# A graph network layer in f32: aggregated rows through DRAM at register-held addresses, and 16 gathers from x in the head

## The chip, the cores and the metric

The kernel runs on one core of a Trainium2 chip. The metric is device time in microseconds of one execution, the median of several. A core has five engines that work from queues of their own: PE (matrix multiplication, PEld being its weight loads), DVE (vector), ACT (activation functions), POOL (GpSimd, which here issues the gathers) and SP (which here only issues DMA transfers and, after the change, loads registers). The engines run in order, each for itself, and wait for one another by semaphores.

## The reference

A message-passing layer over a graph of 6250 nodes with 256 features and 206250 edges. The edges come sorted by their target `dst`. Everything is f32.

```
h   = relu(layernorm(x))                                    # per node
e   = relu(raw @ W_e1.T + b_e1) @ W_e2.T + b_e2             # raw: 64 features per edge
emb = (e * (clip(pol, 0, 1) + 0.01)) @ W_le.T + b_le
msg = relu(h[src] + emb)                                    # a gathered row of h per edge
agg = segment_sum(msg, dst, 6250)
g   = (h + agg) @ W_g1.T + b_g1
out = x + relu(layernorm(g) * ln_g + ln_b) @ W_g2.T + b_g2
```

The edges per node average 33; the sums per node are what the change touches.

## The kernel before

**Edges.** 128 edges are a tile, 4 tiles (512 edges) a *block*, 403 blocks in all; half a block, 256 edges, is a *unit*, 806 in all. Six blocks are a *group* `g` of 3072 edges, 68 groups in all. A group is cut into four *strips* of 768 consecutive edges, and tile `j` of each block belongs to strip `j`. A strip's edges have targets within `W` = 32 consecutive nodes, beginning at the strip's first target, `base_b[:, g, j]`. A test on the chip checks this; where it fails, a general loop (`any_order`, L845) does the layer again at the end.

**Per unit.** `first_layer` (L239, matmul L250, ReLU on ACT L259 and DVE L256) makes the hidden layer of two blocks, `edge_part` (L266, matmul L274) multiplies by the product of the second and third weights, DVE moves the result out of PSUM (`msg`, L279). POOL gathers two tiles of 128 rows of `hb_d` (the normalized nodes with a bias added, in DRAM) into `hg` by indirect DMAs (`gather`, L566). `whole(u)` (L607) then makes the message: DVE multiplies `msg` by the polarity and adds `hg` (L615), ACT takes the ReLU (L620). `add_up` (L622, matmul L632) sums messages into 4 x 32 rows of PSUM per group with a 0/1 matrix; `keep` (L639) copies a finished group's rows to `ms[g]` (L644).

**Per node window.** 128 nodes are a *window* `w`, 49 in all. A window can get rows from two or three groups (`groups_of`, L71). `node_work` (L680) loads x transposed (L691) and its statistics (L693), makes h from them (L707, four DVE instructions), builds one 128 x 128 selection matrix per group (L698), and sums the groups' rows into the window's nodes on PE (L732: two halves of the features, a matmul per group and half), adds them (L734), and goes through `first` (matmul L170, L176), `second` (transposes L186) and `third` (matmul L196, result L198). A matmul in f32 is recorded as two.

**The order** is written out by hand (`manual_schedule`). A loop over the units (L785) places each unit's steps on all engines: `at(u, fn)` puts a step of the node work at a later unit, `steps` and `rest` are small pieces for DVE, taken one per unit by `piece` (L600). PE runs ahead of the gathers: the first `LEAD` = 22 units go through PE while the head still computes `hb_d`, and `whole` follows a lag behind (L793), which starts at `LEAD - RAW` = 18 units and falls by one every `SHRINK` = 44 units. For eight units in a row the sums and first layers are done together (`turn_of`, L291).

**The gathers.** A gather is placed behind a matmul (`in_step`, L578): while the gathers so far times `STEP` = 1.288 are less than the estimated PE time `spent` plus `AFLOAT`. `spent` adds up given costs per step (`EDGE`, `LAYER`, `SUMS`, `NODES`; the last for every step that `due` takes). `whole` places the ones it still lacks with no such wait (L796). There are `HG` = 20 buffers of one unit, and L582 lets no gather go beyond 20 units past those already summed.

**The head** (L355 to 475). Until `hb_d` is written no gather can read it, so the first `RAW` = 4 units gather rows of x itself (8 gathers, L347) and normalize them after gathering (L464, L472, L611 in `whole`). x comes in 13 chunks through 11 buffers (`p1x`), 10 of them asked for at once (`AHEAD`); per chunk DVE takes the statistics (L141, L142), ACT applies them (L388), POOL adds the bias (L392) and SP writes `hb_d` (L394).

Of the kernel before, what the change touches and what calls it, by code (L numbers as in the profile page):

```python
# [17 lines left out]
P = 128  # L18
# [16 lines left out]
NT = NB * S  # L35
NG = NF + 1
NP = -(-NB // 2)
MARGIN = 768
DEG = E // N
LEAD = 22  # L40
# [1 line left out]
EDGE, LAYER, SUMS, NODES = 1.754, 0.9, 0.46, 0.65  # L42
STEP = 1.288
AFLOAT = 6.0
SHRINK = 44
RAW = 4
HG = 16 + RAW
FEW = 6
QUIET = (0, 1)
TURN = 1  # L50
CH = 4
AHEAD = 10
assert DEG * N == E and NF * GE + S * P >= E


# [42 lines left out]
def gnn_kernel(ctx: ExitStack, tc: tile.TileContext, x, src_c, dst_c, dst_r, pol_c, raw_t, w_e1t, w_e2,  # L98
# [50 lines left out]
    def finish_nodes(nd, ps, w, n):  # L149

        r = w * P

        def turn(a):
            pt = ps()
            for c in range(2):
                nc.tensor.transpose(pt[:, 0, c * P:c * P + n], a[:n, c * P:(c + 1) * P], ident[:n, :n])
            aT = nd.tile([P, 2, P], F32, name="aT")
            if n == P:
                nc.scalar.activation(aT, pt[:, 0, :].rearrange("p (c n) -> p c n", c=2), AF.Copy)
            else:  # L160
                for c in range(2):
                    nc.scalar.activation(aT[:, c, :n], pt[:, 0, c * P:c * P + n], AF.Copy)
            return aT

        def first(aT, bias_by_pe=False):
            ph = ps()
            if bias_by_pe:
                nc.tensor.matmul(ph[:n, 0, :], ones[0:1, :n], bg1_b[0:1], start=True, stop=False)
            for c in range(2):
                nc.tensor.matmul(ph[:n, 0, :], aT[:, c, :n], wg1_s[:, c, :], start=c == 0 and not bias_by_pe, stop=c == 1)  # L170
            hs = nd.tile([P, D], F32, name="hs")
            if bias_by_pe:
                hb = ph[:, 0, :]
            else:
                hb = hs
                nc.vector.tensor_add(hs[:n], ph[:n, 0, :], bg1_b[:n])  # L176
            mv = row_stats(nd, n, 1, lambda i: hb[:n])
            rs = nd.tile([P, 1], F32, name="rs1")
            one_over_std(rs[:n], mv, n)
            nc.vector.tensor_scalar(hs[:n], hb[:n], mv[:n, 0, 0:1], rs[:n], op0=ALU.subtract, op1=ALU.mult)  # L180
            return hs

        def second(hs):
            pt = ps()
            for c in range(2):
                nc.tensor.transpose(pt[:, 0, c * P:c * P + n], hs[:n, c * P:(c + 1) * P], ident[:n, :n])  # L186
            nT = nd.tile([P, 2, P], F32, name="nT")
            for c in range(2):
                nc.scalar.activation(nT[:, c, :n], pt[:, 0, c * P:c * P + n], AF.Relu, bias=lnb_s[:, c:c + 1],  # L189
                                     scale=lng_s[:, c:c + 1])  # L190
            return nT

        def third(nT, xt):
            po = ps()
            for c in range(2):
                nc.tensor.matmul(po[:n, 0, :], nT[:, c, :n], wg2_s[:, c, :], start=c == 0, stop=c == 1)  # L196
            ot = nd.tile([P, D], F32, name="ot")
            nc.vector.tensor_add(ot[:n], po[:n, 0, :], xt[:n])  # L198
            for i, (a, b) in enumerate(spread_out(n)):
                eng = nc.scalar if i else nc.sync  # L200
                eng.dma_start(out=out[bass.ds(r + a, b - a), :], in_=ot[a:b])

        def load_x():
            xt = nd.tile([P, D], F32, name="xt3")
            for a, b in spread_out(n):
                nc.sync.dma_start(out=xt[a:b], in_=x[bass.ds(r + a, b - a), :])
# [11 lines left out]
    with fast:  # L218
# [297 lines left out]
        ends = w0.tile([P, 3], F32, name="ends")  # L516
        bad = w0.tile([P, 3], F32, name="bad")
        bad3 = w0.tile([3, 1], F32, name="bad3")

        def by_group(i, op):  # L520
            def step():
# [17 lines left out]

        def count():  # L540
            pq = ps()
            nc.tensor.matmul(pq[:3, 0, 0:1], bad, ones[:, 0:1], start=True, stop=True)
            nc.vector.tensor_copy(bad3, pq[:3, 0, 0:1])

        def total():
            pq = ps()
            nc.tensor.matmul(pq[:1, 0, 0:1], bad3, ones[0:3, 0:1], start=True, stop=True)
            nc.vector.tensor_copy(bad_i, pq[:1, 0, 0:1])


        with tc.tile_pool(name="hg", bufs=HG - RAW) as hg_p, tc.tile_pool(name="ms", bufs=5) as ms_p, \
                tc.tile_pool(name="sel2", bufs=9) as sel2_p, tc.tile_pool(name="nd", bufs=3) as nd:
            got = 2 * RAW
            acc = {}
            made = 0
# [83 lines left out]
            def keep(g):  # L639

                if g is not None:
                    ms[g] = ms_p.tile([P, D], F32, name="ms")
                    if g != NG - 2:
                        nc.scalar.activation(ms[g], acc.pop(g), AF.Copy)  # L644
# [29 lines left out]
            rest = deque()  # L674
            ending = {-2: [], -1: []}

            def at(u, fn):
                todo.setdefault(max(u, now), deque()).append(fn)

            def node_work(w, spread_now=False):  # L680
# [6 lines left out]

                def spread():
                    box["xt"] = load_x()
                    box["hT"] = nd.tile([P, 2, P], F32, name="hT")  # L690
                    nc.sync.dma_start(out=box["hT"][:, :, :n], in_=x_t[:, :, w * P:w * P + n])  # L691
                    st = nd.tile([P, 2, P], F32, name="stb")
# [88 lines left out]
            for i, fn in enumerate((by_group(0, ALU.max), by_group(1, ALU.min), by_row(0, ALU.max), by_row(1, ALU.min),  # L781
                                    verdict, count, total)):
                at(LEAD + 22 + 5 * i, fn)
            flag = None
            for u in range(LEAD, NU):  # L785
# [9 lines left out]
                while made < ready_for:  # L795
                    gathers(made + 1)  # L796
                    whole(made)
                    made += 1
                due()
                if len(rest) > 6:  # L800
                    piece()
                if u == NU - 24:
# [1 line left out]
                        if groups_of(w)[-1] == NG - 1:  # L804
                            late[w] = node_work(w, True)
                if u == LEAD + 60:
                    flag = nc.values_load(bad_i[0:1, 0:1], min_val=0, max_val=3 * P)
            while todo:
                now = min(todo)
                for fn in todo.pop(now):  # L810
                    fn()
            while steps:
                steps.popleft()[1]()
            before, last = ending[-2], ending[-1]
# [192 lines left out]
```

## Time and profile before

| | us |
|---|---|
| median of 3 runs | 2162.19 (2161.35 to 2164.05) |
| the profiled execution, its own time | 2161.02 |
| its span, first to last instruction | 2159.3 |
| busy in the span: PE | 2144.8 |
| busy: DVE, POOL, ACT | 1665.9, 1621.5, 980.5 |
| gathers from `hb_d` (POOL, L566) | 1604, mean 983 ns |
| L732, matmuls that sum groups' rows into windows | 548 records, 69.3 busy |

The profile lists for each group of instructions its line, engine, operation and tiles, the count behind an x, then busy time, mean duration of one in ns, and behind the second bar the engine's idle time just before them with what ended most of it. In a timeline the columns are start and duration in us; in square brackets stands the idle time before and its releaser. Busy time of PE is modelled, and issuing a DMA or loading a register is not counted as busy.

### The profile page before, as it was taken

Reading aid. Unit: us, or ns where it says so; the run is one execution under the profiler, and the core shown is the slowest. Engines: PE = TensorE matmul, PEld = TensorE weight load, DVE = VectorE, ACT = ScalarE, POOL = GpSimd, SP = SyncE. Lnnn points to the kernel's source line nnn. Section 1 sums busy time; section 2 is a strip of 40 time slices with the busy share of each in tenths; the row PEclk is TensorE's granted clock in tenths of the full one; section 3 lists DMA queues with packets and bytes.
Section 4 is the critical chain, followed back from the end, with each engine's and each line's share of the span. In section 5 each row is a group of like instructions: output and inputs, shape, how many; then the busy total and the mean of one; then the engine's idle time right before and its main releaser. Section 6 shows DMA issues by size and latency. Waiting matters only on the chain.

```text
span 2159.3 us, 35666 instructions
## 1 busy us (share of the span) xinstructions
PE 2144.8 (99%) x12382; PEld 1613.3 (75%) x12382; DVE 1665.9 (77%) x3975; ACT 980.5 (45%) x1710; POOL 1621.5 (75%) x1675
## 2 busy tenths in 40 slices
PE   9999999999999999999999999999999999999998
PEld 6677777777777777777777777777777777777776
DVE  7898777877777777777777777778777778777786
ACT  7544444444444444444444444444444444444443
POOL 6777777777777777777777777777777777777773
PEclk9999999999999999999999999999999999999999
DMA  9544454544445454545454445444544554454442
GB/s 312 175 134 127 141 157 135 150 137 131 140 131 148 144 149 125 152 131 149 124 151 142 133 130 153 143 133 141 147 138 125 150 151 140 128 152 131 140 138 73
DMA packets 156227, 309.23 MB, mean 143 GB/s; under 512 B 33328, under 2 KB 78089, under 8 KB 156041
## 3 DMA queue, kind: packets, MB, share of 16 engines
q0 software_dynamic: 77376, 211.39, 34.6%
q1 hardware_dynamic: 77364, 92.23, 13.6%
q10 hardware_dynamic: 1300, 3.28, 0.5%
q8 instruction: 98, 1.61, 0.3%
q14 instruction: 89, 0.72, 0.1%
HBM read 293.92 MB, written 12.85 MB: 142 GB/s over the span
## 4 chain that ended last, share of the span: by engine, by line
PE 96%; DVE 2%; DMA 1%; ACT 0%; issue 0%; SPq 0%; DVEq 0%; ACTq 0%
PE pz L274 64%; PE pz L250 17%; PE pd L632 9%; PE pz L732 3%; PE pz L170 2%; PE pz L196 2%; DMA raw<-in_raw_t_dram 1%; PE pz L186 1%; DVE hg L615 0%; DVE msg L279 0%; DVE st L141 0%; DMA xt<-in_x_dram 0%; DVE sel L595 0%; DVE mvx L142 0%; DVE msg L613 0%
## 5 line engine op out<-in xcount | busy, mean ns | idle before, releaser
L566 POOL DMA_INDIRECT hg<-hb_d,src_s x1604 | 1576.6, 983 | 493.9 <-issue 319.8
L274 PE MATMUL pz<-wc_s,e 128*128 128x256 f32 x6448 | 1452.6, 381 | 0.0
L274 PEld LDWEIGHTS pz<-wc_s,e 128*128 128x128 f32 x6448 | 1209.5, 190 | 235.2 <-ACT e L259 71.3
L620 ACT ACTIVATE hg<-hg 128x512 f32<-128x512 f32 x805 | 507.6, 631 | 862.7 <-DVE hg L615 860.9
L615 DVE SCALAR_TENSOR_TENSOR hg<-msg,pol_s,hg 128x256 f32<-128x256 f32 x1612 | 696.8, 477 | 15.6 <-DMA hg<-hb_d,src_s 14.9
L279 DVE TENSOR_TENSOR msg<-pz,bc_s 128x512 f32<-128x512 f32 x799 | 545.5, 683 | 74.0 <-PE pz L274 73.7
L256 DVE TENSOR_SCALAR e<-pz,vecs 128x512 f32<-128x512 f32 x201 | 150.8, 750 | 361.1 <-PE pz L250 361.0
L259 ACT ACTIVATE e<-pz,vecs 128x512 f32<-128x512 f32 x605 | 361.1, 691 | 148.4 <-PE pz L250 148.3
L250 PE MATMUL pz<-raw,we_s 64*128 64x512 f32 x1612 | 379.3, 604 | 3.7 <-DVE msg L279 2.0
L250 PEld LDWEIGHTS pz<-raw,we_s 64*128 64x128 f32 x1612 | 148.5, 187 | 188.2 <-issue 155.4
L632 PE MATMUL pd<-hg,sel 128*32 128x256 f32 x3216 | 194.9, 382 | 0.6 <-ACT hg L620 0.6
L632 PEld LDWEIGHTS pd<-hg,sel 128*32 128x32 f32 x3216 | 94.4, 109 | 87.8 <-issue 34.9
L595 DVE SCALAR_TENSOR_TENSOR sel<-iota_w,zero_c,rel 128x128 f32<-128x128 f32 x403 | 137.3, 341 | 0.0
L644 ACT ACTIVATE ms<-pd 128x256 f32<-128x256 f32 x66 | 25.2, 382 | 127.2 <-PE pd L632 127.1
L732 PEld LDWEIGHTS pz<-s,ms 128*128 128x128 f32 x548 | 68.7, 192 | 3.1 <-PE pd L632 0.4
L732 PE MATMUL pz<-s,ms 128*128 128x128 f32 x548 | 69.3, 275 | 0.1
L707 DVE SCALAR_TENSOR_TENSOR hT<-hT,zero_c,stb 128x128 f32<-128x128 f32 (+1 forms) x196 | 66.7, 341 | 3.0 <-DMA stb<-st_d 3.0
L196 PE MATMUL pz<-wg_s,nT 128*128 128x256 f32 (+1 forms) x196 | 50.6, 380 | 0.6 <-ACT nT L189 0.6
L170 PE MATMUL pz<-wg_s,hT 128*128 128x256 f32 (+1 forms) x196 | 50.5, 380 | 0.0
L392 POOL TENSOR_TENSOR hb<-xt,rows_b 128x256 f32<-128x256 f32 (+1 forms) x49 | 34.1, 728 | 10.5 <-ACT xt L388 3.0
L196 PEld LDWEIGHTS pz<-wg_s,nT 128*128 128x128 f32 (+1 forms) x196 | 37.0, 190 | 6.2 <-ACT nT L189 0.8
L170 PEld LDWEIGHTS pz<-wg_s,hT 128*128 128x128 f32 (+1 forms) x196 | 37.0, 190 | 5.7 <-issue 0.3
(98 smaller groups left out, 412.8 us busy)
## 6 DMA issues: line engine op xcount, KB each, us to landing
raw<-in_raw_t_dram SPq DMA_DIRECT2D x202, 256.0 KB
hg<-hb_d,src_s POOLq DMA_INDIRECT x1604
stb<-st_d SPq DMA_DIRECT2D x49, 128.0 KB
hb_d<-hb SPq DMA_DIRECT2D x12, 512.0 KB
xt<-in_x_dram SPq DMA_DIRECT2D x48, 128.0 KB
hT<-in_x_t_dram SPq DMA_DIRECT2D x48, 128.0 KB
out_dram<-ot SPq DMA_DIRECT2D x48, 128.0 KB
xt<-in_x_dram SPq DMA_DIRECT2D x11, 512.0 KB
```

The costliest lines, as they stand in the source:

```text
L196: nc.tensor.matmul(po[:n, 0, :], nT[:, c, :n], wg2_s[:, c, :], start=c == 0, stop=c == 1)
L250: z = nc.tensor.matmul(pe[s, c], we1_s[s * F:(s + 1) * F, c * P:(c + 1) * P], raw[q][s * F:(s + 1) * F, :], start=True, stop=True)
L256: nc.vector.tensor_scalar(e1[b][:, c, :], pe[s, c], be1_s[:, c:c + 1], 0.0, op0=ALU.add, op1=ALU.max)
L259: nc.scalar.activation(e1[b][:, c, :], pe[s, c], AF.Relu, bias=be1_s[:, c:c + 1])
L274: last_z = nc.tensor.matmul(pz[:, i, :], e1[b][:, c, k:k + P], wc_s[:, c, :], start=c == 0, stop=c == 1)
L279: nc.vector.tensor_add(msg[u], pz, bc_s)
L566: g = nc.gpsimd.indirect_dma_start(out=hg[u][:, i, :], out_offset=None, in_=hb_d, in_offset=bass.IndirectOffsetOnAxis(ap=src_s[:, 2 * u + ...
L595: nc.vector.scalar_tensor_tensor(sel[g][:, k * S:(k + 1) * S, :], iota_w.rearrange("p (o w) -> p o w", o=1).to_broadcast([P, S, W]), zero_ ...
L615: nc.vector.scalar_tensor_tensor(hg[u][:, i, :], m[:, i, :], pol_s[:, 2 * u + i:2 * u + i + 1], hg[u][:, i, :], op0=ALU.mult, op1=ALU.add)
L620: nc.scalar.activation(hg[u], hg[u], AF.Relu)
L632: z = nc.tensor.matmul(acc[g][j * W:(j + 1) * W, :], sel[g][:, k * S + j, :], m[:, j % 2, :], start=k == 0, stop=b == blocks_of(g)[-1])
L732: nc.tensor.matmul(pa[:, c, :n], ms[g][:, c * P:(c + 1) * P], box["sel2"][i][:, :n], start=i == 0, stop=i == len(gs) - 1)
```

## The change

For the windows whose last group is below `FAR` = 66 (47 of 49) the sums take another way.

- **Rows to DRAM** (`rows_out`). When a group below 66 is finished, SP loads the first rows of its four strips into registers and writes each strip's 32 rows of `ms[g]` to DRAM at that row: strips 0 and 2 to `sum_d[0]`, 1 and 3 to `sum_d[1]`, so that neighbours, which can share nodes, never write the same array. Both arrays are cleared window by window some groups ahead (`clear`, from a tile of zeros). A new term of the test (`strips_apart`) checks that strips two apart begin at least 32 rows apart.
- **Rows back** (`far_work`, instead of `node_work`). Per window: x is loaded one unit after the window's last group, h is made from it on ACT four units after, and the window's 128 rows of both arrays are read; six units after, DVE adds both to h; nine units after, PE transposes the result (two transposes, `turn`, L153) and ACT copies it; then `first`, `second` and `third` as before. Gone for these windows are the selection matrices, L691, L693, L707, L732 and L734.
- **The head.** `RAW` is 8: 16 gathers of x instead of 8, their statistics and normalization with them, and eight gathers from `hb_d` fewer. `HG` stays 20. x goes through 9 buffers instead of 11, 8 asked for at once. The lag starts at 22 - 8 = 14 units and falls by one every 57 units.
- Buffers: `ms` 4 instead of 5, `sel2` 6 instead of 9, new pools for the rest.

```diff
-SHRINK = 44
-RAW = 4
-HG = 16 + RAW
+SHRINK = 57
+RAW = 8
+HG = 20
-AHEAD = 10
+AHEAD = 8
+CLEAR = 4
+FAR = NG - 2
...
+    sum_d = [dram.tile([N + W, D], F32, name=f"sum_d{i}") for i in range(2)]
...
-        def turn(a):
+        def turn(a, pool=nd, name="aT"):
...
-        with tc.tile_pool(name="p1", bufs=4) as p1, tc.tile_pool(name="p1x", bufs=11) as p1x:
+        with tc.tile_pool(name="p1", bufs=4) as p1, tc.tile_pool(name="p1x", bufs=9) as p1x:
...
+            nc.vector.tensor_copy(base_i, base_b[0:1].rearrange("p g j -> p (g j)"))
+            nc.vector.memset(zrow, 0.0)
...
+        def strips_apart():
+            flat = base_b.rearrange("p g j -> p (g j)")
+            n = FAR * S - 2
+            nc.vector.tensor_tensor(apart[:, :n], flat[:, 2:n + 2], flat[:, :n], ALU.subtract)
+            nc.vector.tensor_reduce(ends[:, 3:4], apart[:, :n], axis=AX.X, op=ALU.min)
...
+            nc.vector.tensor_scalar(bad[:, 3:4], ends[:, 3:4], float(W), None, op0=ALU.is_lt)
...
-                if steps and steps[0][0] <= now:
-                    steps.popleft()[1]()
+                due_now = [s for s in steps if s[0] <= now][:1]
+                if due_now:
+                    steps.remove(due_now[0])
+                    due_now[0][1]()
...
+                    if g < FAR:
+                        soon(1, lambda: rows_out(g, 0))
+                        soon(2, lambda: rows_out(g, 1))
                     for w in range(NW):
-                        if groups_of(w)[-1] == g:
+                        if groups_of(w)[0] == g + CLEAR:
+                            soon(6, lambda w=w: clear(w))
+                        if groups_of(w)[-1] == g < FAR:
+                            far_work(w)
+                        elif groups_of(w)[-1] == g:
                             late.pop(w)()
-                        elif groups_of(w)[-1] == g + 1 < NG - 1:
+                        elif groups_of(w)[-1] == g + 1 == FAR:
                             late[w] = node_work(w)
...
+            def soon(n, fn):
+                moves.setdefault(now + n, []).append(fn)
+
+            def clear(w):
+                if groups_of(w)[-1] < FAR:
+                    for i in range(2):
+                        nc.sync.dma_start(out=sum_d[i][w * P:(w + 1) * P, :], in_=zrow)
+
+            def rows_out(g, k):
+                if k == 0:
+                    _, firsts[g] = nc.values_load_multi_w_load_instructions(
+                        base_i[0:1, g * S:(g + 1) * S], engines=[mybir.EngineType.SP], min_val=0, max_val=N)
+                for i in range(2):
+                    j = 2 * k + i
+                    nc.sync.dma_start(out=sum_d[i][bass.ds(firsts[g][j], W), :], in_=ms[g][j * W:(j + 1) * W, :])
+
+            def far_work(w):
+                box = {}
+                turn, first, second, third, load_x, offset = finish_nodes(nd, ps, w, P)
+
+                def h_of_x():
+                    box["xt"] = load_x()
+                    box["h"] = nh.tile([P, 2, P], F32, name="stb").rearrange("p a b -> p (a b)")
+
+                def load():
+                    nc.scalar.activation(box["h"], box["xt"], AF.Relu, bias=nm_s[:, w:w + 1], scale=rs_s[:, w:w + 1])
+                    box["ab"] = ab_p.tile([P, 2, D], F32, name="ab")
+                    for i in range(2):
+                        nc.sync.dma_start(out=box["ab"][:, i, :], in_=sum_d[i][w * P:(w + 1) * P, :])
+
+                def add(i):
+                    nc.vector.tensor_add(box["h"], box["h"], box["ab"][:, i, :])
+
+                def turned():
+                    box["hT"] = turn(box["h"], nh, "hT")
+                    at(now + 2, one)
...
+                soon(1, h_of_x)
+                soon(4, load)
+                steps.extend((now + 6, lambda i=i: add(i)) for i in range(2))
+                steps.extend((now + 7, lambda c=c: offset(box["xt"], c)) for c in range(2))
+                at(now + 9, turned)
...
+            now = LEAD
+            for w in range(NW):
+                if groups_of(w)[0] < CLEAR:
+                    soon(8, lambda w=w: clear(w))
...
                 due()
+                for fn in moves.pop(now, []):
+                    fn()
```

More of the change, by code (lines that the diff above doesn't have):

```diff
@@ L156, in turn @@
                 nc.tensor.transpose(pt[:, 0, c * P:c * P + n], a[:n, c * P:(c + 1) * P], ident[:n, :n])
-            aT = nd.tile([P, 2, P], F32, name="aT")
+            aT = pool.tile([P, 2, P], F32, name=name)
             if n == P:
@@ L512, in row_numbers @@
                 nc.vector.tensor_scalar(rowid[q], base_b[q, :, j], p32[q], None, op0=ALU.add)
+            nc.vector.tensor_copy(base_i, base_b[0:1].rearrange("p g j -> p (g j)"))
+            nc.vector.memset(zrow, 0.0)
         far = w0.tile([P, 2, NG], F32, name="far")
-        ends = w0.tile([P, 3], F32, name="ends")
-        bad = w0.tile([P, 3], F32, name="bad")
-        bad3 = w0.tile([3, 1], F32, name="bad3")
+        ends = w0.tile([P, 4], F32, name="ends")
+        bad = w0.tile([P, 4], F32, name="bad")
+        bad4 = w0.tile([4, 1], F32, name="bad4")
+        apart = w0.tile([P, FAR * S], F32, name="apart")
         def by_group(i, op):
@@ L538, in verdict @@
             nc.vector.tensor_scalar(bad[:, 2:3], ends[:, 2:3], float(GE // 2 + MARGIN), None, op0=ALU.is_gt)
+            nc.vector.tensor_scalar(bad[:, 3:4], ends[:, 3:4], float(W), None, op0=ALU.is_lt)
         def count():
             pq = ps()
-            nc.tensor.matmul(pq[:3, 0, 0:1], bad, ones[:, 0:1], start=True, stop=True)
-            nc.vector.tensor_copy(bad3, pq[:3, 0, 0:1])
+            nc.tensor.matmul(pq[:4, 0, 0:1], bad, ones[:, 0:1], start=True, stop=True)
+            nc.vector.tensor_copy(bad4, pq[:4, 0, 0:1])
         def total():
             pq = ps()
-            nc.tensor.matmul(pq[:1, 0, 0:1], bad3, ones[0:3, 0:1], start=True, stop=True)
+            nc.tensor.matmul(pq[:1, 0, 0:1], bad4, ones[0:4, 0:1], start=True, stop=True)
             nc.vector.tensor_copy(bad_i, pq[:1, 0, 0:1])
-        with tc.tile_pool(name="hg", bufs=HG - RAW) as hg_p, tc.tile_pool(name="ms", bufs=5) as ms_p, \
-                tc.tile_pool(name="sel2", bufs=9) as sel2_p, tc.tile_pool(name="nd", bufs=3) as nd:
+        with tc.tile_pool(name="hg", bufs=HG - RAW) as hg_p, tc.tile_pool(name="ms", bufs=4) as ms_p, \
+                tc.tile_pool(name="sel2", bufs=6) as sel2_p, tc.tile_pool(name="ab", bufs=2) as ab_p, \
+                tc.tile_pool(name="nh", bufs=2) as nh, tc.tile_pool(name="nd", bufs=3) as nd, \
+                tc.tile_pool(name="nk", bufs=1) as nk:
+            base_i = nk.tile([1, NG * S], I32, name="base_i")
+            zrow = nk.tile([P, D], F32, name="zrow")
             got = 2 * RAW
@@ L675, in gnn_kernel, with one, two @@
             ending = {-2: [], -1: []}
+            moves = {}
+            firsts = {}
+            def soon(n, fn):
[27 more added lines that the diff above has]
+                    at(now + 2, one)
+                def one():
+                    box["hs"] = first(box["hT"])
+                    at(now + 5, two)
+                def two():
+                    box["nT"] = second(box["hs"])
+                    at(now + 4, lambda: third(box["nT"], box["xt"]))
+                soon(1, h_of_x)
[3 more added lines that the diff above has]
+                at(now + 9, turned)
             def at(u, fn):
@@ L689, in spread @@
                     box["xt"] = load_x()
-                    box["hT"] = nd.tile([P, 2, P], F32, name="hT")
+                    box["hT"] = nh.tile([P, 2, P], F32, name="hT")
                     nc.sync.dma_start(out=box["hT"][:, :, :n], in_=x_t[:, :, w * P:w * P + n])
-                    st = nd.tile([P, 2, P], F32, name="stb")
+                    st = nh.tile([P, 2, P], F32, name="stb")
                     nc.sync.dma_start(out=st, in_=st_d[w:w + 1].to_broadcast([P, 2, P]))
@@ L806, in gnn_kernel @@
                 if u == LEAD + 60:
-                    flag = nc.values_load(bad_i[0:1, 0:1], min_val=0, max_val=3 * P)
+                    flag = nc.values_load(bad_i[0:1, 0:1], min_val=0, max_val=4 * P)
             while todo:
@@ L811, in gnn_kernel @@
                     fn()
+            assert not moves
             while steps:
```

2 lines of the change are left out of this document (1 added, 1 removed).

## The prediction

> **What bounds the kernel now.** I read the page first, then a table of the middle (200 to 2000 us), the groups of instructions, the timelines of POOL, DVE and PE.
>
> ```profile
> span 2159.3 us, 35666 instructions
> ...
> PE 2144.8 (99%) x12382; PEld 1613.3 (75%) x12382; DVE 1665.9 (77%) x3975; ACT 980.5 (45%) x1710; POOL 1621.5 (75%) x1675
> ...
> PE 96%; DVE 2%; DMA 1%; ACT 0%; issue 0%; SPq 0%; DVEq 0%; ACTq 0%
> ...
> L566 POOL DMA_INDIRECT hg<-hb_d,src_s x1604 | 1576.6, 983 | 493.9 <-issue 319.8
> ...
> L615 DVE SCALAR_TENSOR_TENSOR hg<-msg,pol_s,hg 128x256 f32<-128x256 f32 x1612 | 696.8, 477 | 15.6 <-DMA hg<-hb_d,src_s 14.9
> ```
>
> ```profile
> 200.00:2000.00 1800.00, 1800.00 (x10502) 1359.66 (x10501) 1379.22 (x3260) 805.71 (x1388) 1372.90 (x1401) 1.00 0.48 140
> ```
>
> PE looks like the only bound: no idle time in the middle, 96% of the chain. POOL shows 75%. But its 1401 gathers took 1800 us, one per 1.285 us, and a timeline shows what the busy share hides:
>
> ```profile
> 7.80 0.95 POOL L347 DMA_INDIRECT hg<-in_x_dram,src  x1 [0.30 <-issue]
> 9.06 0.95 POOL L347 DMA_INDIRECT hg<-in_x_dram,src  x1 [0.30 <-issue]
> ...
> 65.31 0.98 POOL L566 DMA_INDIRECT hg<-hb_d,src_s  x1 [3.00 <-DMA raw<-in_raw_t_dram]
> 66.59 0.95 POOL L566 DMA_INDIRECT hg<-hb_d,src_s  x1 [0.30 <-issue]
> 69.00 1.56 POOL L566 DMA_INDIRECT hg<-hb_d,src_s  x1 [1.46 <-PE pz L274]
> ...
> 98.17 0.95 POOL L566 DMA_INDIRECT hg<-hb_d,src_s  x1 [0.30 <-issue]
> ...
> 301.52 0.95 POOL L566 DMA_INDIRECT hg<-hb_d,src_s  x1 [0.30 <-issue]
> ...
> 1003.66 0.94 POOL L566 DMA_INDIRECT hg<-hb_d,src_s  x1 [0.30 <-ACT hg L620]
> 1004.91 0.95 POOL L566 DMA_INDIRECT hg<-hb_d,src_s  x1 [0.30 <-issue]
> ...
> 2131.85 0.95 POOL L566 DMA_INDIRECT hg<-hb_d,src_s  x1 [0.30 <-issue]
> ```
>
> 0.95 us and a gap of 0.30 is a gather's cadence when nothing holds POOL (9.06 - 7.80 in the head), and it is the cadence in the middle too, whoever is named as releaser. The group agrees: 493.9 us of idle time is 1604 gaps of 0.30 (481) and 13 us more. So **POOL is full from 65.31 to 2132.80** (2131.85 + 0.95): 2067.5 us for 1604 gathers, 1.289 each.
>
> The Trainium skill, "Perfetto Trace Analysis", section "GPSIMD Engine Instruction", says to time such instructions by the spacing of their starts, not by their reported duration. By duration (1596 x 0.983 = 1569 us) POOL would have 500 us to spare and the second case below would hold; by spacing it has almost none, and the rows agree with that.
>
> How much does POOL have to spare? From a gather's end to its use, and at the very end:
>
> ```profile
> 304.29 0.48 DVE L615 SCALAR_TENSOR_TENSOR hg<-msg,pol_s,hg 128x256 f32<-128x256 f32 x1 [0.44 <-DMA hg<-hb_d,src_s]
> ```
>
> ```profile
> L615 DVE SCALAR_TENSOR_TENSOR hg<-msg,pol_s,hg x1612: 466/477/552, 71.7 to 2143.9; 128x256 f32<-128x256 f32 x180
> ```
>
> The gather that began at 301.52 ended at 302.47; DVE, which was waiting, went on at 304.29: landing takes 1.82 us. The last gather was used 2143.9 - 2132.8 = 11.1 us after its end, so POOL ends **9.3 us** before it would hurt. After that use the kernel needs 2159.3 - 2143.9 = 15.4 us whatever came before.
>
> **The change part by part.**
>
> PE. Windows 0 to 46 (47 of 49) lose their sums at L732 and get two transposes each.
>
> ```profile
> 337.27 1.50 PE L732 MATMUL pz<-s,ms 128*128 128x128 f32 x12
> 338.61 1.68 PE L274 MATMUL pz<-wc_s,e 128*128 128x256 f32 x7
> ```
>
> ```profile
> 297.17 0.38 PE L186 MATMUL pz<-ident,hs 128*128 128x128 f32 x2
> 297.39 1.89 PE L274 MATMUL pz<-wc_s,e 128*128 128x256 f32 x8
> ```
>
> Twelve L732 records occupy 338.61 - 337.27 = 1.34 us, 0.112 each. The 47 windows have 134 (window, group) pairs, each of two halves recorded as two passes: 536 records, 59.9 us. A transpose occupies 0.22 / 2 = 0.11 us: 94 of them, 10.3 us. PE's own work shrinks by **49.6 us**, all of it on the chain.
>
> DVE and ACT.
>
> ```profile
> L707 DVE SCALAR_TENSOR_TENSOR hT<-hT,zero_c,stb 128x128 f32<-128x128 f32 (+1 forms) x196 | 66.7, 341 | 3.0 <-DMA stb<-st_d 3.0
> L698 DVE TENSOR_SCALAR s<-iota_p,rowid 128x128 f32<-128x128 f32 x140 | 31.6, 289 | 0.0
> L734 DVE SCALAR_TENSOR_TENSOR hT<-hT,pz 128x256 f32<-128x256 f32 x48 | 19.6, 409 | 0.0
> L176 DVE TENSOR_TENSOR hs<-pz,rows_b 128x256 f32<-128x256 f32 x47 | 19.5, 414 | 0.0
> L644 ACT ACTIVATE ms<-pd 128x256 f32<-128x256 f32 x66 | 25.2, 382 | 127.2 <-PE pd L632 127.1
> L472 ACT ACTIVATE hg<-hg,nm,rs 128x256 f32<-128x256 f32 x8 | 4.0, 587 | 0.5 <-DVE nm L468 0.5
> L611 DVE TENSOR_TENSOR hg<-hg,rows_b 128x512 f32<-128x512 f32 x4 | 2.7, 680 | 0.0
> ```
>
> A far window loses 2.85 x 0.226 (31.6 / 140) + 4 x 0.340 + 0.41 = 2.4 us of DVE and gains two adds, by L176 0.83: 74 us less of 1665.9. ACT gains one scaled ReLU (0.59) and one copy out of PSUM (0.38): 46 us on 980.5. Neither engine bounds the middle before or after; both cost nothing there.
>
> SP. Per group (2159 / 68 = 32 us): four registers and four writes of 32 KB; per window two clears and two reads of 128 KB, for two loads fewer.
>
> ```profile
> L807 SPq TENSOR_LOAD <-bad_i x1: 485/485/485, 216.8 to 216.8; - x1
> L807 SPq FUSED_REGOPS  x1: 181/181/181, 217.3 to 217.3; - x1
> ```
>
> ```profile
> 57.25 4.83 SPq L394 DMA_DIRECT2D hb_d<-hb  x4
> ...
> 314.72 0.42 SPq L206 DMA_DIRECT2D xt<-in_x_dram  x1
> ```
>
> A register costs about 0.7 us, an issue 0.42: 66 x 2.8 + 452 x 0.42 = 375 us over the run, on a queue that mostly waits. The DMA engines move 264 x 32 KB and 94 x 128 KB more, 21 MB beside 140 GB/s x 2159 us = 302 MB, at a share of 0.48: 7% more on engines that are half idle. The way through DRAM: registers 2.8 us, two rounds of writes, of which the second may wait for the first to land, then the read. Nothing shows a write read back at once; the nearest is the last write of hb_d (issued by 62.08) and the first gather from it (65.31): at most 3.2 us. So 2.8 + 3 x 3.2 = 12.4 us and some issues; below, with no waits between them, about 8. The add is put six units after the group, and a unit is two gathers: 6 x 2 x 1.285 = 15.4 us. I take the cover as enough and the cost as nothing; behind a late add DVE could not evacuate PSUM, and PE would stop.
>
> POOL. Eight of the gathers from hb_d move into the head: 1596 x 1.289 instead of 1604, **10.3 us** less. It pays back in the head:
>
> ```profile
> 54.43 6.41 POOL L392 TENSOR_TENSOR hb<-xt,rows_b 128x256 f32<-128x256 f32 x9 [1.56 <-issue]
> ```
>
> ```profile
> 60.35 0.42 DVE L141 BATCH_NORM_STATS2 st<-hg 128x6 f32<-128x256 f32 x1
> 60.80 0.18 DVE L142 BATCH_NORM_AGGREGATE mv<-st 128x2 f32<-128x6 f32 x1
> 61.02 0.43 DVE L141 BATCH_NORM_STATS2 st<-hg 128x6 f32<-128x256 f32 x1
> ...
> 83.01 0.75 DVE L256 TENSOR_SCALAR e<-pz,vecs 128x512 f32<-128x512 f32 x1 [1.69 <-PE pz L250]
> ```
>
> ```profile
> 98.02 2.78 PE L632 MATMUL pd<-hg,sel 128*32 128x256 f32 x44
> ```
>
> (a) The second gather began at 7.80, so the sixteenth ends at 7.80 + 14 x 1.25 + 0.95 = 26.3, 10 us later than the eighth did. But POOL's adds for hb had gaps: 49 of them at 0.71 (6.41 / 9) in a row would end at 61.2, where they ended at 60.84. The first gather slips by 0 to 2 us; I take 0.7, and 0.3 for the one behind PE. (b) The limit at L582 is 20 units, 40 gathers, until the first sums (98.02). Before, 32 of them came from hb_d; now 24. Row 98.17 is the 24th: POOL runs out just as the sums come. And the sums come later: eight more row statistics at 0.67 (61.02 - 60.35) and four more L611 make 8.1 us on a DVE that idled some 3.4 us there (1.69 of it in the row above): 4.7 us. The first pair's sums take 1 us, so POOL, done at 100.1 (99.1 before, and (a)), goes on at 103.7: 3.3 us lost beyond (a), as I reckon the last gap of 0.3 into the cadence; ends 0 and 6. The loads of x are asked for later, two chunks at a time, but were ready over 10 us before their use; nothing, ends 0 and 2.
>
> **The sum.** PE alone: 2161.0 - 49.6 + 4.7 = 2116.1. POOL: last gather ends at 2132.8 - 10.3 + 1.0 + 3.3 = 2126.8; plus 1.8 and 15.4 is a span of 2144.0. The greater holds: **POOL becomes the bound**. With the 1.7 us around the span (2161.02 - 2159.3) that is 2145.7 for a profiled run, and with the 1.2 us by which the median of before (2162.19) stands over its profiled run, **2147 us**. Of PE's 49.6 us some 30 come back as waits of DVE for gathers.
>
> **The rivals.**
>
> 1. PE stays the bound, at 2116 + 1 = 2117 us: the gather's cadence would have to fall from 1.289 to 1.27 (PE's 30 us over 1596). For it: the least is 1.25. Against: the middle kept 1.285 for 1800 us. The Trainium skill, "SBUF — State Buffer", section "Who interferes with whom", says that a DVE tensor_scalar in a two-port mode shuts GpSimd out for its whole length, which would leave gathers shorter once 134 of L698 are gone. By L698's row that is at most 134 x 0.226 = 30 us, just this case. No row here shows a gather blocked by L698. Chance 0.10.
>
> 2. POOL is held by PE: gathers are paced behind matmuls, by the code's costs. Each window has one paced step less and the lag is shorter, so the same gather is issued nearer to its use; counted in program order the lead falls from about 3 units early to none by the middle. Then POOL waits where PE does its sums and first layer. If each of some 30 turns (gathers 500 to 1000) costs POOL half a microsecond, 2162; I take 2157 to 2168. Against: POOL, being late, finds most matmuls done. Chance 0.18.
>
> 3. Slower: the sums come back from DRAM too late and DVE stands at the add, with it PE. Place: 47 adds. Each late microsecond costs up to 47 us on PE's 2117: it passes POOL's 2147 at 0.64 us each, and before at 0.96. At 2 us each (a way of 17.4 us instead of 12.4) it gives 2211. Speaking against: the way above. Chance 0.11.
>
> 4. The change doesn't do what it says: two strips two apart begin under 32 rows from each other and the general loop runs as well, over 1600 more gathers of 1.25, beyond 4100 us. A strip has 768 edges, about 23 rows, two 46. Chance 0.01.
>
> **How the numbers follow.** The forecast has 0.60. Its own range: head costs 0 instead of 4.3 and a cadence 0.5% shorter (8 us), 2135; as much longer and the head's upper ends, 2160. The range goes 5 us lower for a part of the first rival (a sixth of its 30 us) and up to the end of the second: 2130 to 2168. That leaves out 0.20, the rest of the first, and the third beyond 2168 with the fourth. A measurement here can tell about 0.2%, 4.3 us: faster is below 2157.9, slower above 2166.5. Faster: 0.57 of the forecast, 0.10, 0.07 of the second: 0.74. Same: 0.03, 0.08 of the second, 0.02 of the third: 0.13. Slower: 0.03 of the second, 0.09, 0.01: 0.13.
>
> **What would show it.** Right: about 1596 gathers from hb_d that still take 1.28 to 1.29 each from 66 on; a last use at L615 about 1.8 us after the last gather's end; DVE's waits for hg grown from 14.9 us to several tens; PE with 1 to 2% idle in the middle, L732 gone but for 12 records; one gap on POOL of a few us near 100. Wrong: PE still without idle time and the end near 2116; gaps on POOL in the middle behind PE; DVE waiting for the tile read back from DRAM.

## The result, and the profile after

The changed kernel takes **2305.22 us** (median of 4 runs, 2302.06 to 2307.21) against 2161.95 for the kernel before on the same chip: a ratio of **1.0659, 95% interval 1.0641 to 1.0678**. The forecast was 2147. It is slower by 143 us, and none of the forecast's own steps says where these are.

The page of the changed kernel (its lines are numbered anew: L253, L277, L584, L635, L640 and L652 were L250, L274, L566, L615, L620 and L632):

```profile
span 2301.7 us, 36220 instructions
...
PE 2184.1 (95%) x11940; PEld 1597.5 (69%) x11940; DVE 1646.6 (72%) x3725; ACT 1012.6 (44%) x1812; POOL 1602.9 (70%) x1675
...
PE   8899999999999999999999998988988898888998
...
POOL 7677777777777777777777775666656565566575
PEclk9899999999999999999999999999989898999999
...
L584 POOL DMA_INDIRECT hg<-hb_d,src_s x1596 | 1550.8, 972 | 668.4 <-issue 388.7
```

The digits (40 slices of 57.5 us) show a kernel of two halves: for 24 slices POOL stands at 7 as before, then mostly at 5 or 6, and PE loses its full 9s. The gathers did not get longer (972 ns); POOL's idle time grew from 493.9 to 668.4 us. 1596 gaps of 0.305 are 487, so **some 180 us are gaps beyond the cadence**: some 14 in the head, nearly all the rest after 1000 us. A table of stretches (busy us and count for PE, PEld, DVE, ACT and POOL, then granted clock, DMA share, GB/s) says the same:

```profile
200.00:1000.00 800.00, 798.20 (x4555) 594.74 (x4555) 607.05 (x1371) 378.65 (x671) 609.25 (x627) 1.00 0.51 151
1400.00:2200.00 800.00, 716.51 (x3718) 515.20 (x3715) 509.40 (x1111) 306.50 (x546) 493.77 (x515) 0.94 0.42 124
```

627 gathers in 800 us at first, one per 1.28 us, as forecast; then 515, one per 1.55. What one turn of eight units looks like there, on POOL and then on PE:

```profile
1960.30 0.94 POOL L584 DMA_INDIRECT hg<-hb_d,src_s  x1 [9.81 <-PE pz L253]
1961.54 0.95 POOL L584 DMA_INDIRECT hg<-hb_d,src_s  x1 [0.30 <-issue]
...
1979.09 0.95 POOL L584 DMA_INDIRECT hg<-hb_d,src_s  x1 [0.30 <-issue]
1989.30 0.95 POOL L584 DMA_INDIRECT hg<-hb_d,src_s  x1 [9.26 <-ACT e L262]
```

```profile
1963.92 3.62 PE L277 MATMUL pz<-wc_s,e 128*128 128x256 f32 x16
1973.30 2.07 PE L173 MATMUL pz<-wg_s,hT 128*128 128x256 f32 x4 [5.77 <-ACT hT L162]
...
1979.40 5.34 PE L277 MATMUL pz<-wc_s,e 128*128 128x256 f32 x24
1984.67 1.93 PE L652 MATMUL pd<-hg,sel 128*32 128x256 f32 x32
1986.53 3.70 PE L253 MATMUL pz<-raw,we_s 64*128 64x512 f32 x16
```

POOL does a turn's sixteen gathers in a row (1960.30 to 1980.04) and then stands for 9.26 us, until PE has been through the sums (L652) and part of the first layers (L253): the next gather is placed behind them. (The profile infers the releaser: it names PE's L253 at one of the two gaps and, at the other, ACT's L262, which reads what L253 wrote.) PE in its turn stood for 5.77 us ahead of L173 while those gathers ran. Why for gathers, when ACT's copy hT is named? ACT and DVE just ahead of it:

```profile
1969.84 0.63 ACT L640 ACTIVATE hg<-hg 128x512 f32<-128x512 f32 x1 [1.82 <-DVE hg L635]
...
1972.35 0.63 ACT L640 ACTIVATE hg<-hg 128x512 f32<-128x512 f32 x1 [1.18 <-DVE hg L635]
1972.89 0.36 ACT L162 ACTIVATE hT<-pz 128x256 f32<-128x256 f32 x1
```

```profile
1971.77 0.48 DVE L635 SCALAR_TENSOR_TENSOR hg<-msg,pol_s,hg 128x256 f32<-128x256 f32 x1 [0.68 <-DMA hg<-hb_d,src_s]
```

The copy (L162) is queued behind the ReLU of a message (L640), that behind DVE's L635, and that waited for its gather. So the two engines wait for each other in turn: a turn takes 29.0 us (1960.30 to 1989.30), of which POOL uses 20 and PE 23. The groups of the whole run:

```profile
L635 DVE SCALAR_TENSOR_TENSOR hg<-msg,pol_s,hg 128x256 f32<-128x256 f32 x1612 | 732.7, 480 | 377.6 <-DMA hg<-hb_d,src_s 373.2
...
L173 PE MATMUL pz<-wg_s,hT 128*128 128x256 f32 (+1 forms) x196 | 65.0, 463 | 66.7 <-ACT hT L162 66.7
...
L741 DVE TENSOR_TENSOR stb<-stb,ab 128x256 f32<-128x256 f32 x94 | 39.4, 419 | 1.7 <-DMA ab<-sum_d 1.7
```

DVE's waits for gathers went from 14.9 to 373.2 us. The adds of the sums read back from DRAM (L741) waited 1.7 us in all, twice in 94 times: that way is in time.

### The profile page after: what moved, and what is told of

Its sections match the earlier page's. It is cut to its first block, busy times and chain, and to the rows that moved or that the text cites. A ratio compares the mean times of both kernels' runs of the same rounds, so it can differ in the third digit from the quotient of the medians.

```text
span 2301.7 us, 36220 instructions
## 1 busy us (share of the span) xinstructions
PE 2184.1 (95%) x11940; PEld 1597.5 (69%) x11940; DVE 1646.6 (72%) x3725; ACT 1012.6 (44%) x1812; POOL 1602.9 (70%) x1675
## 5 line engine op out<-in xcount | busy, mean ns | idle before, releaser
L584 POOL DMA_INDIRECT hg<-hb_d,src_s x1596 | 1550.8, 972 | 668.4 <-issue 388.7
L277 PE MATMUL pz<-wc_s,e 128*128 128x256 f32 x6448 | 1476.7, 385 | 0.0
L277 PEld LDWEIGHTS pz<-wc_s,e 128*128 128x128 f32 x6448 | 1228.5, 193 | 246.6 <-ACT e L262 76.3
L640 ACT ACTIVATE hg<-hg 128x512 f32<-128x512 f32 x805 | 507.4, 630 | 1138.1 <-DVE hg L635 1133.6
L635 DVE SCALAR_TENSOR_TENSOR hg<-msg,pol_s,hg 128x256 f32<-128x256 f32 x1612 | 732.7, 480 | 377.6 <-DMA hg<-hb_d,src_s 373.2
L253 PE MATMUL pz<-raw,we_s 64*128 64x512 f32 x1612 | 418.3, 624 | 25.8 <-DVE msg L282 18.4
L262 ACT ACTIVATE e<-pz,vecs 128x512 f32<-128x512 f32 x605 | 361.4, 693 | 73.6 <-PE pz L253 73.1
L253 PEld LDWEIGHTS pz<-raw,we_s 64*128 64x128 f32 x1612 | 160.8, 190 | 233.5 <-issue 123.1
L652 PE MATMUL pd<-hg,sel 128*32 128x256 f32 x3216 | 200.7, 382 | 11.9 <-ACT hg L640 11.9
L652 PEld LDWEIGHTS pd<-hg,sel 128*32 128x32 f32 x3216 | 95.3, 109 | 104.1 <-issue 34.9
L173 PE MATMUL pz<-wg_s,hT 128*128 128x256 f32 (+1 forms) x196 | 65.0, 463 | 66.7 <-ACT hT L162 66.7
L173 PEld LDWEIGHTS pz<-wg_s,hT 128*128 128x128 f32 (+1 forms) x196 | 40.2, 222 | 83.7 <-ACT hT L162 77.2
L741 DVE TENSOR_TENSOR stb<-stb,ab 128x256 f32<-128x256 f32 x94 | 39.4, 419 | 1.7 <-DMA ab<-sum_d 1.7
L192 ACT ACTIVATE nT<-pz,vecs 128x128 f32<-128x128 f32 (+1 forms) x98 | 38.7, 444 | 2.5 <-PE pz L189 2.5
L214 DVE SCALAR_TENSOR_TENSOR xt<-xt,zero_c,rows_b 128x128 f32<-128x128 f32 (+1 forms) x98 | 33.5, 342 | 0.0
```

The source lines that it names most:

```text
L253: z = nc.tensor.matmul(pe[s, c], we1_s[s * F:(s + 1) * F, c * P:(c + 1) * P], raw[q][s * F:(s + 1) * F, :], start=True, stop=True)
L262: nc.scalar.activation(e1[b][:, c, :], pe[s, c], AF.Relu, bias=be1_s[:, c:c + 1])
L277: last_z = nc.tensor.matmul(pz[:, i, :], e1[b][:, c, k:k + P], wc_s[:, c, :], start=c == 0, stop=c == 1)
L584: g = nc.gpsimd.indirect_dma_start(out=hg[u][:, i, :], out_offset=None, in_=hb_d, in_offset=bass.IndirectOffsetOnAxis(ap=src_s[:, 2 * u + ...
L635: nc.vector.scalar_tensor_tensor(hg[u][:, i, :], m[:, i, :], pol_s[:, 2 * u + i:2 * u + i + 1], hg[u][:, i, :], op0=ALU.mult, op1=ALU.add)
L640: nc.scalar.activation(hg[u], hg[u], AF.Relu)
```

## The experiments

**Theory (pacing).** The code places gathers behind matmuls by an account (`spent`, L578): so many us credited per step, 1.288 asked per gather. A window of the 47 has four credited steps instead of five, 0.65 each. Adding the code's own costs, the account ends at some 2041 us instead of 2071, while 1596 gathers need 1596 x 1.288 = 2055.6. The gathers are placed later and later. Counted in program order, by 200 gathers each, the mean distance in units between a gather's place and its use (its *lead*) is about 4, 3, 2, 1, 0.7, 0, 0 and 2 in the changed kernel and 3.5 to 6 in the one before. Without distance, a gather behind the turn's sums can't begin until PE is there, and PE can't go on until the gather has landed.

**Rivals.** (A) ACT's copy of the transposed rows, L162, which the groups name ahead of PE. (B) The new traffic through DRAM or the new work as such. (C) The 16 gathers of x in the head.

**The wait taken away (free).** In the changed kernel gathers keep their places but no longer wait for a matmul.

```diff
-                    gather(behind)
+                    gather()
```

> The changed kernel with one thing taken away: a gather is no longer placed behind a matmul (the pacing wait of in_step); buffers and data waits stay. Pacing theory (the gathers have lost their lead in program order, so POOL stands behind matmuls that stand behind DVE's wait for gathers): POOL's 166 us of gaps after the head go, the gathers run at 1.28 each, 2135 to 2150 us. Rival, the copy of hT (PE stands at L173 for ACT's copy L162, some 77 us, since the first product comes two units after the transposes): PE's waits there stay, 2230 us or more. Rival, the way through DRAM: about 2300, nothing changes.

Measured 2148.18 us, ratio 0.9934 (0.9917 to 0.9951). Its groups:

```profile
L584 POOL DMA_INDIRECT hg<-hb_d,src_s x1596 | 1566.6, 982 | 496.5 <-issue 331.8
...
L635 DVE SCALAR_TENSOR_TENSOR hg<-msg,pol_s,hg 128x256 f32<-128x256 f32 x1612 | 715.7, 481 | 179.5 <-DMA hg<-hb_d,src_s 177.2
...
L173 PE MATMUL pz<-wg_s,hT 128*128 128x256 f32 (+1 forms) x196 | 52.9, 393 | 10.6 <-ACT hT L162 10.4
```

and its middle:

```profile
200.00:2000.00 1800.00, 1790.17 (x10233) 1331.71 (x10230) 1353.56 (x3059) 848.45 (x1497) 1372.56 (x1404) 1.00 0.50 151
```

One line is worth 157 us. POOL's idle time falls by 172 us (its gathers get 16 us longer), and PE is busy for 1790 of 1800. The DRAM way, the transposes and the head are all still there, so (B) and (C) can't be the 157 by themselves; and PE's wait for the copy falls from 66.7 to 10.4 us with the copy left where it was, which speaks against (A).

**The same wait in the kernel before (free_before).** The same edit there, as a control.

> The kernel before without the pacing wait. Its gathers never stood behind a matmul for more than their own gap of 0.3 us after the head, so pacing cost nothing there: 2158 to 2166 us by the pacing theory as by all others; a control. Faster than that would mean that pacing cost time before too.

Measured 2160.8, ratio 0.9998 (0.9989 to 1.0008). With a lead of about four units the wait costs nothing.

**The account mended (credit).** The wait stays; a window's four steps are credited as much as its five were.

```diff
-EDGE, LAYER, SUMS, NODES = 1.754, 0.9, 0.46, 0.65
+EDGE, LAYER, SUMS, NODES = 1.754, 0.9, 0.46, 0.8125
```

> The changed kernel with NODES 0.8125 instead of 0.65: the four paced steps of a far window add as much to the PE time that paces the gathers as the five of the kernel before. Counted in program order the gathers' lead is then 5 to 9 units throughout, instead of 4 falling to 0. All waits keep their form. Pacing theory: the gaps on POOL behind matmuls vanish, 2135 to 2150 us, the same as without pacing. Rival, the copy of hT: about 2230 to 2300. Rival, the way through DRAM: about 2300.

Measured 2150.27, ratio 0.9946 (0.9929 to 0.9962); the lead, counted as above, is about 5 to 10 units.

```profile
200.00:2000.00 1800.00, 1789.90 (x10218) 1329.81 (x10215) 1354.59 (x3059) 846.86 (x1496) 1372.19 (x1405) 1.00 0.50 151
```

The row can hardly be told from that of the kernel without the wait. So the wait itself does no harm; the account does.

**The kernel before with a wrong account (tight_before).** None of the change, but each gather is charged more.

```diff
-STEP = 1.288
+STEP = 1.308
```

> The kernel before with STEP 1.308 instead of 1.288, nothing else: its gathers are asked for more slowly, and counted in program order their lead falls from 3 units to 0 by gather 500 and stays there, as in the changed kernel's last half. No sums go through DRAM and no transposes are added. Pacing theory: gaps on POOL behind matmuls at the units where sums and first layers come together, 2230 to 2350 us. Copy theory and DRAM theory: 2162 to 2180 us.

Measured 2268.92 (one run), as expected, 5% above before, from a constant that adds no instruction.

```profile
200.00:400.00 200.00, 200.00 (x1191) 150.66 (x1191) 152.30 (x360) 87.42 (x151) 151.23 (x155) 1.00 0.47 140
400.00:1600.00 1200.00, 1163.89 (x6357) 848.19 (x6354) 854.49 (x1984) 485.35 (x846) 820.16 (x848) 0.98 0.43 128
1600.00:2000.00 400.00, 400.00 (x2341) 302.03 (x2340) 308.78 (x727) 179.33 (x311) 305.68 (x310) 1.00 0.47 139
```

The loss comes and goes. From 400 to 1600 us POOL does 848 gathers, one per 1.42 us. From 1600 on it is back at 1.29 (310 in 400), because by then the account is so short that nearly every gather (by the count 192 of the fifth 200, 199 of the sixth, and then all) is placed by `whole`, without a wait. It hurts where gathers behind matmuls have no lead, not where the account is shortest and they have no wait.

**PE's copy given more time (later_one).** In the changed kernel the first product comes five units behind the transposes instead of two. Rival (A) wants most of the loss back.

```diff
-                    at(now + 2, one)
+                    at(now + 5, one)
```

> The changed kernel with the first product of a far window five units after its transposes instead of two, so that ACT's copy of hT is done. Copy theory: PE's 67 to 77 us of waiting at L173 go, and the time with them, about 2230 us. Pacing theory: these waits are a consequence of late gathers; they go at L173 but come back elsewhere, 2270 to 2305 us, POOL's gaps over 120 us.

Measured 2342.67 (one run): slower still, and above what I had put for pacing.

```profile
L173 PE MATMUL pz<-wg_s,hT 128*128 128x256 f32 (+1 forms) x196 | 50.6, 381 | 1.4 <-ACT hT L162 1.4
```

The waits named in the changed kernel are gone (66.7 to 1.4 us), and POOL's gaps of over 0.60 us add up to 216 us beyond the cadence, where the changed kernel has 179. (A) falls: the largest wait on PE's list was a place where waiting shows, not its cause. Why this order costs 37 us more was not settled.

**Each part alone.** head_only is the kernel before with the 16 gathers of x in the head; dram_only is the changed kernel with the old head. For head_only, on the kernel before,

```diff
-SHRINK = 44
-RAW = 4
-HG = 16 + RAW
+SHRINK = 57
+RAW = 8
+HG = 20
-AHEAD = 10
+AHEAD = 8
```

and for dram_only, on the changed kernel,

```diff
-SHRINK = 57
-RAW = 8
+SHRINK = 44
+RAW = 4
-AHEAD = 8
+AHEAD = 10
```

with 9 and 11 buffers for `p1x`.

> The kernel before with only the second part of the change: RAW 8, HG 20, SHRINK 57, 8 loads of x at once, 9 buffers; the sums stay on PE. Counted in program order the gathers' lead is 5 to 9 units throughout. Pacing theory: no gaps on POOL but the one in the head; PE stays the bound, its head some 5 to 10 us later than before (DVE's eight extra statistics, a late load of raw): 2162 to 2174 us. If the second part itself were at fault: 2250 us or more.

> The changed kernel with only the first part: rows through DRAM, but RAW 4, lag 18 falling by one in 44, 10 loads of x at once, 11 buffers as before. The lead in program order falls from 3 units to 0 by gather 600 and stays there. Pacing theory: gaps behind matmuls from about 500 us on, with the first part alone: 2230 to 2330 us. If both parts were needed for the loss: under 2180 us.

head_only: 2175.26, ratio 1.0066 (1.0049 to 1.0083), 1 us beyond the end of what was expected. Its middle:

```profile
200.00:2000.00 1800.00, 1800.00 (x10490) 1358.25 (x10486) 1375.40 (x3251) 806.04 (x1388) 1375.29 (x1395) 1.00 0.47 140
```

PE bounds it, so it shows what the new head costs PE: 2175.26 - 2161.28 = **14 us**, for a forecast of 4.7. (11.1 of them lie ahead of the first sums, 109.08 for 98.02 us before; the rest comes later.) dram_only: 2239.39 (one run), as expected.

```profile
200.00:500.00 300.00, 298.14 (x1727) 220.91 (x1727) 226.25 (x511) 140.22 (x248) 228.71 (x235) 1.00 0.50 152
500.00:1500.00 1000.00, 939.44 (x5114) 685.88 (x5110) 690.12 (x1526) 419.46 (x748) 680.19 (x706) 0.97 0.45 137
1500.00:2000.00 500.00, 496.80 (x2841) 370.83 (x2842) 376.80 (x847) 234.24 (x415) 381.07 (x391) 1.00 0.51 152
```

The first part alone brings the loss, at 500 to 1500 us, where the lead goes through zero earlier than in the full change; afterwards it recovers as tight_before did. That the full change is 66 us slower still fits the same count: its 1596 gathers need 2055.6 us of the account where 1604 need 2066.0, so its lead runs out later, and 46 of its seventh 200 gathers and 12 of the last 196 are still placed behind a matmul, in dram_only none. No run tests this by itself.

**The first part without the wait (dram_free), and a head between the two (raw6_free).** dram_free is dram_only with the edit of free. raw6_free is the same with `RAW` 6, `SHRINK` 50, `AHEAD` 9 and ten buffers.

> The first part alone as in the run before it, and without the pacing wait. POOL as the bound: 65.3 + 1604 gathers of 1.285 to 1.289, then 17.2 for the end and 1.7 around the span: 2146 to 2152 us, the same as the whole change without pacing (2148), since the eight gathers saved in the head were paid back there. If the head's part is worth its 10 us: 2158 us.

> Rows through DRAM, no pacing wait, and 12 gathers from x in the head (RAW 6, lag 16 falling by one in 50, 9 loads of x at once, 10 buffers). POOL as the bound, against the version with 8 gathers from x (2138.6): four gathers from hb_d fewer, 5.1 us, a start about 1 us later, and a gap on POOL at the first sums of 0 to 2 us, since 28 gathers last until about 103 us and the first sums come near 103: 2134 to 2139 us. If the gap is as with 16 gathers (8.9 us): 2143 us.

dram_free: 2138.59, ratio 0.9899 (0.9883 to 0.9916), 7 us below the lower end of what was expected. raw6_free: 2137.66, ratio 0.9885 (0.9869 to 0.9902), as expected and not to be told from dram_free. These are the best versions here: the sums through DRAM are worth 1.0 to 1.2% once the wait is out of the way. The second part brings nothing: with 12 gathers of x the time is the same, and with 16 (free, 2148.18) it is 10 us longer. It takes gathers from a POOL that is full, but makes POOL stand in the head. In dram_free POOL runs from first gather to last:

```profile
66.20 0.98 POOL L584 DMA_INDIRECT hg<-hb_d,src_s  x1 [2.26 <-DVE st L144]
...
2117.87 0.95 POOL L584 DMA_INDIRECT hg<-hb_d,src_s  x1 [0.31 <-issue]
```

That is 2052.6 us for 1604 gathers, 1.280 each, without a gap above 0.32 us.

**Is POOL the bound there? (eighth.)** dram_free with every eighth gather replaced by a plain load of as many other rows, issued by SP. It leaves out an eighth of the gathering, so the messages of those tiles are not the reference's.

```diff
+                if u % 4 == 3 and i == 1:
+                    r = 61 * u % 6000
+                    nc.sync.dma_start(out=hg[u][:, i, :], in_=hb_d[r:r + P, :])
+                    return
```

> The version with rows through DRAM, 8 gathers from x and no pacing wait; every eighth gather from hb_d is replaced by a plain load of 128 rows by SP, other rows than those wanted, so the messages of those tiles are wrong; the work of all other engines is the same. POOL as the bound: with 12% of its gathers gone POOL has some 250 us to spare and the time falls to PE's own, 2161.0 - 49.6 and 1 to 3 for the head and the median: 2111 to 2120 us, with PE without idle time in the middle. If PE or the way through DRAM were the bound of that version: 2135 to 2142 us.

Measured 2112.35, ratio 0.9773 (0.9757 to 0.9789), as expected.

```profile
200.00:2000.00 1800.00, 1800.00 (x10374) 1342.03 (x10374) 1355.18 (x3082) 859.26 (x1510) 1218.59 (x1252) 1.00 0.51 154
```

PE is without idle time again, as in the kernel before, and the time falls by 26 us more. POOL, at three quarters busy, was the bound of dram_free; 2112 is what PE itself needs.

## Why the prediction was wrong, point by point

**The step that failed** is the price of the second rival. I named the mechanism, the paced steps and the lead that falls "from about 3 units early to none by the middle", and then priced it: "If each of some 30 turns (gathers 500 to 1000) costs POOL half a microsecond, 2162". And I argued it down: "Against: POOL, being late, finds most matmuls done." The runs showed some 30 turns with waits, from 1397 us on (about gather 1015, where I had gathers 500 to 1000), but at **5 us each** instead of 0.5: some 155 of the 166 us of gaps after the head. No row carried the half microsecond. The argument against it took POOL's lateness for a cover, but PE then waits for the gathers and is late itself, so the matmul in question is always still to come. With no lead the two engines take turns, and their times add. Half a microsecond was a token; a price was to be had from the order of the work, in which a gather placed behind the sums and first layers has to sit through most of them. In the rows of PE above these two take 5.6 us of a turn (1984.67 to 1990.23), so 30 turns are 168 us, and 2147 + 168 would have been 2315. That is hindsight, and the closeness is partly chance, since the gaps of single turns run from under 1 to nearly 10 us; but it is the term that was missing.

**POOL becomes the bound, 2147.** This sum was right for the kernel without the wait: 2148.18 measured; the last gather ended at 2129.6 for 2126.8, and the span was 2146.6 for 2144.0. That it came within 3 us is partly luck: the head made it 7.4 us later than summed (below), and a gather took 1.286 us instead of 1.289, 4.6 us less over 1596. One part of the sum failed there too: of PE's 49.6 us some 30 were to come back as DVE's waits for gathers, and in free these are 177.2 us, while PE idles only 10 of 1800 us. The full queue behind a busy share of 75% was read rightly, too. "Perfetto Trace Analysis" of the Trainium skill, section "GPSIMD Engine Instruction", would have instructions of GpSimd timed by the spacing of their starts; the run with an eighth fewer gathers agrees with it, being 26 us faster though POOL was nominally a quarter idle.

**PE -49.6 us.** Kept: from 2161.24 to 2112.35 with the old head and POOL out of the way, -48.9. The forecast for PE alone, 2117, contained this and a head of +4.7; measured it would be 2112 and +14, so 2126 (a sum of two runs, not a run).

**The way through DRAM in time.** Right (L741, 1.7 us). A piece of it was oversized: I took 0.7 us for a register. The rows of SP, with first and last start (counts, then minimum, median and maximum in ns):

```profile
L719 SPq FUSED_REGOPS  x264: 147/152/178, 117.1 to 2268.5; - x132
...
L719 SPq TENSOR_LOAD <-base_i x66: 294/300/640, 116.6 to 2267.3; - x66
```

```profile
L723 SPq FUSED_REGOPS  x264: 37/42/48, 118.2 to 2272.4; - x132
L723 SPq MOVE sum_d<-ms x264: 12/29/86, 118.4 to 2272.4; - x132
L723 SPq DMA_DIRECT2D sum_d<-ms x264: 314/343/1821, 118.5 to 2272.5; - x132
```

Loading a group's four registers (L719) took 0.30 us for the load and 0.15 us of register work for each, some 0.9 us or 0.23 a register. A write at a row held in a register (L723) then cost 0.07 us of register work and 0.34 us of issue, and SP was no limit. The third rival, 47 late adds, did not happen; the time ended on its side for another reason.

**The head.** Undersized throughout. In the changed kernel:

```profile
39.95 3.54 PE L253 MATMUL pz<-raw,we_s 64*128 64x512 f32 x8 [4.58 <-DMA raw<-in_raw_t_dram]
86.05 2.07 PE L253 MATMUL pz<-raw,we_s 64*128 64x512 f32 x2 [2.84 <-ACT base_b L494]
110.05 2.37 PE L652 MATMUL pd<-hg,sel 128*32 128x256 f32 x40
```

```profile
67.84 0.98 POOL L584 DMA_INDIRECT hg<-hb_d,src_s  x1 [2.03 <-DVE mv L145]
...
98.05 1.12 POOL L584 DMA_INDIRECT hg<-hb_d,src_s  x1 [5.78 <-PE pz L277]
...
112.33 0.94 POOL L584 DMA_INDIRECT hg<-hb_d,src_s  x1 [1.45 <-ACT hg L640]
```

And in free:

```profile
68.39 0.98 POOL L584 DMA_INDIRECT hg<-hb_d,src_s  x1 [1.96 <-DVE mv L145]
...
110.81 0.99 POOL L584 DMA_INDIRECT hg<-hb_d,src_s  x1 [8.90 <-ACT st_s L509]
```

The first sums came at 110.05 for 98.02 before, 12.0 us later where I had 4.7. Two of its parts I had put at nothing or not seen: a load of raw 4.58 us late, and PE 2.84 us behind ACT's L494, which comes after the sixteen normalizations in its queue. The gap on POOL when the buffers run out, ahead of the 25th gather from `hb_d`, was 8.90 us in free (8.6 beyond the usual gap), for 3.3; with the first gather at 68.39 for 66.3 that is the 7.4 us. In the changed kernel the same gap, at 112.33, was only 1.45, because POOL had already stood behind matmuls in the head: the 5.78 us at 98.05 are ahead of the 15th gather, with buffers left.

**Signs.** "Gaps on POOL in the middle behind PE" stood among what would show me wrong, and is what the trace showed. Of the signs for right, the cadence (1.28 to 1.29) held up to 1000 us, and the matmuls of L732 shrank to 12 records. A gap of a few us came near 100 us, but behind a matmul and not for want of buffers.

**The first rival** (shorter gathers, PE as the bound) did not happen. "SBUF — State Buffer" of the Trainium skill, section "Who interferes with whom", lets DVE's tensor_scalar block GpSimd when it runs in a two-port mode; 134 of 140 such L698 went. With the same head, the mean gather went from 983 to 975 ns (before, dram_free) and from 988 to 982 (head_only, free): 10 to 13 us over 1600 gathers, of the 30 I had allowed. The sign is the rule's; but two kernels that differ by the pacing wait alone, with L698 in both, stand at 983 and 987, and no run takes L698 away by itself. This stays open, and with it why dram_free was 7 us better than expected.

## What to carry to other kernels

When a queue is paced by an account of another engine's work, a change that removes credited steps changes the pacing: add up what the account will credit and what the queue needs, before anything else. Two engines that wait for each other with no lead do not hide one another; price such a turn at the whole stretch that one stands behind, not at a token share. The largest named wait is where the shortage shows; to find its cause, look for the gaps on the engine that should be full.

## What was not expected of the hardware

The granted clock went down with PE's idle time although that came in short pieces like the 5.77 us above: 1.00 where PE was busy for 798 of 800 us, 0.94 where for 717 of 800. The matmuls were slower too: in the changed kernel PE's 11940 records are 2184.1 us of busy time, in free 2113.5. How much of this is the clock was not separated. In the second half a gather still took 0.94 to 0.95 us, with 0.30 between two where POOL did not wait: the whole loss lay between gathers, none of it in them.
